# One stream of strips for the end of a four-layer image model on Trainium2

## The chip, the cores and the metric

The kernel runs on one core of a Trainium2 chip. A core has a matrix engine (TensorE, PE in the profile), a vector engine (VectorE, DVE), an activation engine (ScalarE, ACT), a general one (GpSimd, POOL) and a sync engine (SyncE, SP) that here only issues transfers. Each works through its own queue in order; waits between them go through semaphores. TensorE writes its results to PSUM, here in banks of 512 fp32 columns; all else lies in SBUF, and large tensors in DRAM. The metric is device microseconds of one execution. Before the change the median of three runs is 26510.6 us (26507.2 to 26526.69).

## The reference

The input x has 8 images of 64 x 64 positions and 192 channels. Four layers run one after the other, each with a residual. The last two and the end of the second are what matters:

```python
def _gn(v, G=32, eps=1e-5):
    ...
    m = jnp.mean(g, axis=(1, 2, 4), keepdims=True)
    s = jnp.var(g, axis=(1, 2, 4), keepdims=True)
    return ((g - m) / jnp.sqrt(s + eps)).reshape(v.shape)

def _ss2d(...):                       # layer 1
    ...
    y = out_y[:, 0] + inv_y[:, 0] + wh_y + invwh_y
    ...
    y = (y - mu) * jax.lax.rsqrt(var + 1e-05) * out_norm_w + out_norm_b
    y = y * jax.nn.silu(z)
    return jnp.einsum('bhwd,cd->bhwc', y, out_proj_w)

x = x + _L1_conv_ref(_gn(x), ...)
x = x + _L2_conv_ref(_gn(x), L2_conv_w, L2_conv_b)
x = x + _L3_conv_ref(_gn(x), L3_conv_w, L3_conv_b)
```

Layers 2 and 3 are depthwise 3 x 3 convolutions (each channel has nine taps of its own), of the input normalised over an image and a group of six channels. All is fp32.

## The kernel before

Channels lie on partitions: 192 are two tiles (ct) of 96, the 384 inner channels of layer 1 three tiles (o) of 128. An image has 4096 positions, worked in strips of 512, that is eight image rows (NCH = 8 strips per image, 64 in all). layer0 is layer 0; layer1 calls layer1_in (projection, convolution), layer1_scan (the selective scan in four directions, whose results y go to DRAM) and layer1_out; layers23 is layers 2 and 3. layer0, layer1_in and layer1_scan have a written order: inside every_engine the instructions of the four engines stand as the code emits them, and together runs Python generators in turns, each to its next yield. layer1_out and layers23 are not under it; a scheduler orders them. SP's order is a scheduler's everywhere.

layer1_out takes a strip at a time. It loads four y (L1140), adds them (L1142 and L1144 on VectorE, L1143 on POOL), normalises each row (norm_rows, from L116: bn_stats, Sqrt, subtract and multiply, transposes L137, scale and bias L138), projects the normalised input again for the gate (L1152, Silu L1159), multiplies (L1160), projects out (L1164), adds the residual (L1167) and takes the statistics for layer 2 (L1168). The result x2 goes to DRAM from POOL's queue (L1169). The tables of Sqrt and Silu are in different sets, so ScalarE loads tables twice per strip.

layers23 takes an image at a time. Per layer: group_norm_affine (two tiny matmuls, Sqrt), a normalised copy of the whole image (L1207), then conv3x3 per channel tile. In conv3x3 the three taps with dx = 0 are matmuls with diagonal matrices (L52, L57), the residual a matmul with the identity (L54); ScalarE evicts each strip with the bias (L64), and then VectorE adds the six other taps, each over the whole image (L71). For layer 3, bn_stats run over the finished layer 2 (L1202). At the end the image is turned back by transposes (L1220), copied (L1222, L1224) and stored (L1225).

Of the kernel before, what the change touches and what calls it, by code (L numbers as in the profile page):

```python
# [10 lines left out]
AF = mybir.ActivationFunctionType  # L11
ALU = mybir.AluOpType
PSUM = bass.MemoryType.PSUM
# [3 lines left out]
L = H * W  # L17
CP, CT = 96, 2
DIN = 384
# [19 lines left out]
def img(t, ct):  # L39
    return t[:, ct, :].rearrange("p (h w) -> p h w", w=W)  # L40


def conv3x3(nc, psum, src, dst, w, bias, diag, nct, ident, resid=None):


    rows = NJ // W
    P = src.shape[0]
    for ct in range(nct):
        for r in range(H // rows):
            h0 = r * rows  # L50
            ps = mk(psum, [128, NJ], "mm")[:P]
            nc.tensor.matmul(ps, diag[:, ct, 1, :], src[:, ct, h0 * W : h0 * W + NJ], start=True, stop=False)  # L52
            if resid is not None:
                nc.tensor.matmul(ps, ident[:P, :P], resid[:, ct, h0 * W : h0 * W + NJ], start=False, stop=False)  # L54
            for dy in (-1, 1):
                lo, hi = max(h0, -dy), min(h0 + rows, H - dy)
                nc.tensor.matmul(  # L57
                    ps[:, (lo - h0) * W : (hi - h0) * W],
                    diag[:, ct, 1 + dy, :],
                    src[:, ct, (lo + dy) * W : (hi + dy) * W],  # L60
                    start=False,
                    stop=dy == 1,
                )
            nc.scalar.activation(dst[:, ct, h0 * W : h0 * W + NJ], ps, AF.Identity, bias=bias[:, ct : ct + 1])  # L64
        s, d = img(src, ct), img(dst, ct)
        for dy in (-1, 0, 1):
            for dx in (-1, 1):
                h0, h1 = max(0, -dy), H - max(0, dy)
                w0, w1 = max(0, -dx), W - max(0, dx)
                tap = 3 * (dy + 1) + dx + 1  # L70
                nc.vector.scalar_tensor_tensor(  # L71
                    d[:, h0:h1, w0:w1],
                    s[:, h0 + dy : h1 + dy, w0 + dx : w1 + dx],
                    w[:, ct, tap : tap + 1],
                    d[:, h0:h1, w0:w1],
                    ALU.mult,
                    ALU.add,
                )


# [33 lines left out]


def norm_rows(nc, pool, psum, xt, ident, out, lw, lb):  # L116

    P, nct = out.shape[0], out.shape[1]
    nt = xt.shape[1]
    st = mk(pool, [128, nt, 6], "ln_st")  # L120
    mv = mk(pool, [128, nt, 2], "ln_mv")
    rs = mk(pool, [128, nt], "ln_rs")
    for i in range(nt):
        nc.vector.bn_stats(st[:, i, :], xt[:, i, :])
        nc.vector.bn_aggr(mv[:, i, :], st[:, i, :])
    nc.vector.tensor_scalar(rs, mv[:, :, 1], EPS, None, ALU.add)
    nc.scalar.activation(rs, rs, AF.Sqrt)
    nc.vector.reciprocal(rs, rs)
    for i in range(nt):
        nc.vector.tensor_scalar(  # L130
            xt[:, i, :], xt[:, i, :], mv[:, i, 0:1], rs[:, i : i + 1], ALU.subtract, ALU.mult
        )
    for g in range(nt // 4):
        for ct in range(nct):
            ps = mk(psum, [128, NJ], "tp")[:P]
            for j in range(4):
                nc.tensor.transpose(ps[:, j * 128 : (j + 1) * 128], xt[:, 4 * g + j, ct * P : (ct + 1) * P], ident)  # L137
            nc.scalar.activation(  # L138
                out[:, ct, g * NJ : (g + 1) * NJ],
                ps,  # L140
                AF.Identity,
                bias=lb[:, ct : ct + 1],
                scale=lw[:, ct : ct + 1],
            )
# [571 lines left out]
def layer1(ctx: ExitStack, tc, a, dr, x1, mv1, x2, mv2, cst):  # L716
# [34 lines left out]
    layer1_out(tc, load, w_in, normed, yk, x2, mv2, cst)  # L751
# [372 lines left out]
@with_exitstack  # L1124
def layer1_out(ctx: ExitStack, tc, load, w_in, normed, yk, x2, mv2, cst):

    nc = tc.nc
    ident = cst[0]
    onw, onb = load("onw", [DP, DT]), load("onb", [DP, DT])
    w_out = load("w_out1", [DP, DT, C])  # L1130
    po = ctx.enter_context(tc.tile_pool(name="o1", bufs=2))
    pt = ctx.enter_context(tc.tile_pool(name="t1", bufs=4, space=PSUM))
    for b in range(B):
        stt = mk(po, [CP, CT, NCH, 6], "stt")
        for ch in range(NCH):
            t0 = ch * NJ
            yin = []
            for k in range(K1):
                v = mk(po, [128, NJ // 128, DIN], "yin", bufs=8)
                nc.sync.dma_start(v, yk[b][k][t0 : t0 + NJ, :].rearrange("(t q) d -> q t d", q=128))  # L1140
                yin.append(v)
            nc.vector.tensor_tensor(yin[0], yin[0], yin[1], ALU.add)  # L1142
            nc.gpsimd.tensor_tensor(yin[2], yin[2], yin[3], ALU.add)  # L1143
            nc.vector.tensor_tensor(yin[0], yin[0], yin[2], ALU.add)  # L1144
            yn = mk(po, [DP, DT, NJ], "yn")
            norm_rows(nc, po, pt, yin[0], ident, yn, onw, onb)
            xt, gx = normed(po, b, ch)
            zs = mk(po, [DP, DT, NJ], "zs")
            for o in range(DT):
                ps = mk(pt, [128, NJ], "tp")  # L1150
                for ct in range(CT):
                    nc.tensor.matmul(  # L1152
                        ps,
                        w_in[:, ct, DIN + o * 128 : DIN + (o + 1) * 128],
                        gx[:, ct, :],
                        start=ct == 0,
                        stop=ct == CT - 1,
                    )
                nc.scalar.activation(zs[:, o, :], ps, AF.Silu)  # L1159
            nc.vector.tensor_tensor(zs, zs, yn, ALU.mult)  # L1160
            for ct in range(CT):
                ps = mk(pt, [128, NJ], "tp")[:CP]
                for o in range(DT):
                    nc.tensor.matmul(  # L1164
                        ps, w_out[:, o, ct * CP : (ct + 1) * CP], zs[:, o, :], start=o == 0, stop=o == DT - 1
                    )
                nc.vector.tensor_tensor(xt[:, ct, :], xt[:, ct, :], ps, ALU.add)  # L1167
                nc.vector.bn_stats(stt[:, ct, ch, :], xt[:, ct, :])  # L1168
            nc.gpsimd.dma_start(x2[b][:, :, ch * NJ : (ch + 1) * NJ], xt)  # L1169
        for ct in range(CT):  # L1170
            nc.vector.bn_aggr(mv2[:, b, ct, :], stt[:, ct, :, :])


@with_exitstack
def layers23(ctx: ExitStack, tc, a, x2, mv2, out, cst):
    nc = tc.nc
    ident, _, _, _, grp = cst
    wp = ctx.enter_context(tc.tile_pool(name="w2", bufs=1))
    ws, bs, dgs = [], [], []
    for i in (2, 3):  # L1180
        w = mk(wp, [CP, CT, 9], f"w{i}")
        nc.sync.dma_start(w, a[f"L{i}_w"])
        bt = mk(wp, [CP, CT], f"b{i}")
        nc.sync.dma_start(bt, a[f"L{i}_b"])
        ws.append(w)
        bs.append(bt)
        dgs.append(make_diag(nc, wp, w, CT, ident, f"dg{i}"))
    big = ctx.enter_context(tc.tile_pool(name="big2", bufs=5))
    small = ctx.enter_context(tc.tile_pool(name="small2", bufs=2))
    psum = ctx.enter_context(tc.tile_pool(name="ps2", bufs=4, space=PSUM))  # L1190
    for b in range(B):
        xc = mk(big, [CP, CT, L], "x")
        for ct in range(CT):
            nc.sync.dma_start(xc[:, ct, :], x2[b][:, ct, :])
        mv = mv2[:, b, :, :]
        for i in range(2):
            if i:
                st = mk(small, [CP, CT, NCH, 6], "st")
                mv = mk(small, [CP, CT, 2], "mv")
                for ct in range(CT):  # L1200
                    for ch in range(NCH):
                        nc.vector.bn_stats(st[:, ct, ch, :], xc[:, ct, ch * NJ : (ch + 1) * NJ])  # L1202
                    nc.vector.bn_aggr(mv[:, ct, :], st[:, ct, :, :])
            sc, nb = group_norm_affine(nc, small, psum, mv, grp)
            xn = mk(big, [CP, CT, L], "x")
            for ct in range(CT):
                nc.scalar.activation(  # L1207
                    xn[:, ct, :], xc[:, ct, :], AF.Identity, bias=nb[:, ct : ct + 1], scale=sc[:, ct : ct + 1]
                )
            xo = mk(big, [CP, CT, L], "x")  # L1210
            conv3x3(nc, psum, xn, xo, ws[i], bs[i], dgs[i], CT, ident, resid=xc)
            xc = xo
# [99 lines left out]
```

## Time and profile before

| | |
|---|---|
| median of three runs | 26510.6 us |
| the profiled execution | 26508.04 us |
| its span, first to last instruction | 26506.2 us |
| mean granted TensorE clock over it | 0.942 |
| busy: PE, DVE, ACT, POOL | 90%, 84%, 76%, 66% |
| last operation of the scan on VectorE | about 23664 us |
| last strip of layer1_out done | about 24959 us |

The profile is of one execution. In a line of groups stand the source line, engine and operation, the tiles written and read, the shapes and the number of instructions, then busy time, mean ns of one, and the idle time of the engine just before them with what ended it. A line of waits has who waited, for whom, the total in us, how often, and the longest. A line of the timeline has the start and the length in us and how many instructions were merged; the bracket is the idle time before it. An fp32 matmul of 512 columns shows as two records. PEclk is the clock that TensorE was granted, as a share of full speed; DMA is the mean busy share of the 16 DMA engines.

### The profile page before, as it was taken

The numbers are of one execution on the slowest core, as the hardware profiler recorded it, in microseconds if no ns is written. First come the engines' busy times: TensorE is split into PE (matmuls) and PEld (weight loads), VectorE is DVE, ScalarE is ACT, GpSimd is POOL, SyncE is SP. The second block draws the span as 40 slices with busy tenths as digits, with TensorE's granted clock in tenths as the row PEclk, the third lists the DMA queues.
The fourth block names the chain that finished last, engine by engine and source line by source line (L and its number), as shares of the span: only waits on it lengthen the run. The fifth ranks groups of instructions, "written<-read, shape, count | busy, mean of one in ns | idle before, by whom it ended". The sixth has DMA issues, their size and how long they took to land.

```text
span 26506.2 us, 442347 instructions
## 1 busy us (share of the span) xinstructions
PE 23817.3 (90%) x156160; PEld 18514.6 (70%) x156160; DVE 22196.4 (84%) x25001; ACT 20110.0 (76%) x40019; POOL 17618.6 (66%) x18396
## 2 busy tenths in 40 slices
PE   7888888887799999999999999999999999987766
PEld 4444444444478888888888888888888888863322
DVE  6777777655589999999999999999999999986566
ACT  4555555433379999999999999999999999984322
POOL 2222222210079999999999999999999999972100
PEclk8888888888899999999999999999999999998878
DMA  1111111112233333333333333333333333346411
GB/s 55 42 43 43 42 43 42 34 44 89 90 103 97 94 102 96 95 101 96 96 100 98 94 101 97 96 99 98 95 99 99 95 98 97 96 137 198 126 34 29
DMA packets 1461962, 2275.55 MB, mean 86 GB/s; under 512 B 247181, under 2 KB 773133, under 8 KB 1458202
## 3 DMA queue, kind: packets, MB, share of 16 engines
q1 hardware_dynamic: 1445402, 2196.90, 28.2%
q0 software_dynamic: 14336, 50.34, 0.5%
q8 instruction: 1232, 20.19, 0.3%
q14 instruction: 992, 8.13, 0.1%
HBM read 1811.37 MB, written 435.42 MB: 85 GB/s over the span
## 4 chain that ended last, share of the span: by engine, by line
PE 36%; ACT 29%; DVE 13%; POOL 13%; issue 6%; DMA 2%; POOLq 0%; SPq 0%; DVEq 0%; ACTq 0%
ACT dA L1039 12%; POOL hc L1089 10%; PE pd L1045 6%; ACT sb L1023 6%; PE yt L978 5%; DVE h L1080 5%; ACT bd L1023 4%; PE y L643 3%; PE fc L677 3%; DVE x L71 2%; DVE u L823 2%; PE mm L793 2%; DMA yin<-y 2%; PE pd L1047 2%; PE mm L399 2%
## 5 line engine op out<-in xcount | busy, mean ns | idle before, releaser
L1089 POOL TENSOR_TENSOR hc<-h,bc 128x512 f32<-128x512 f32 x12288 | 15425.9, 1289 | 488.7 <-DVE h L1080 342.0
L1080 DVE TENSOR_TENSOR_SCAN h<-dA,st,pd 128x512 f32<-128x512 f32 x10752 | 12949.9, 1263 | 530.9 <-PE pd L1045 369.4
L1039 ACT ACTIVATE dA<-dl,A_logs 128x512 f32<-128x512 f32 x12288 | 8787.0, 715 | 46.9 <-DVE h L1080 39.6
L978 PE MATMUL yt<-sq,hc 128*128 128x128 f32 x49152 | 7488.5, 275 | 198.8 <-POOL hc L1089 97.3
L1045 PE MATMUL pd<-bd,dut 128*128 128x128 f32 x49152 | 6582.1, 277 | 254.4 <-DVE h L1080 232.1
L1045 PEld LDWEIGHTS pd<-bd,dut 128*128 128x128 f32 x49152 | 5969.2, 192 | 610.3 <-PE yt L978 343.0
L978 PEld LDWEIGHTS yt<-sq,hc 128*128 128x128 f32 x49152 | 5668.1, 141 | 642.1 <-POOL hc L1089 623.3
L1023 ACT ACTIVATE sb<-dut,xt 128x384 f32<-128x384 f32 x8192 | 4763.5, 606 | 1.1 <-DVE dut L964 1.0
L1047 PE MATMUL pd<-sq,sb 128*128 128x128 f32 x24576 | 3739.5, 275 | 9.1 <-DVE h L1080 0.2
L1047 PEld LDWEIGHTS pd<-sq,sb 128*128 128x128 f32 x24576 | 2820.9, 141 | 480.6 <-DVE dl L951 380.8
L1023 ACT ACTIVATE bd<-sq,xt 128x128 f32<-128x128 f32 x8192 | 3011.1, 393 | 0.0
L1080 DVE TENSOR_TENSOR_SCAN h<-dA,pd 128x512 f32<-128x512 f32 x1536 | 1772.6, 1204 | 114.8 <-PE pd L1045 75.6
L71 DVE SCALAR_TENSOR_TENSOR x<-x,w,x 96x3969 f32<-96x3969 f32 (+1 forms) x192 | 838.3, 4366 | 488.6 <-ACT x L64 485.6
L538 POOL TENSOR_TENSOR xdt<-xb,dtv 128x384 f32<-128x384 f32 x256 | 220.7, 862 | 1365.5 <-ACT xb L532 1365.5
L800 POOL COPY xa<-xa 128x192 f32<-128x192 f32 x56 | 19.9, 356 | 1387.9 <-ACT xa L797 1387.9
L413 POOL COPY halo<-raw 128x12 f32<-128x12 f32 x64 | 12.8, 201 | 1380.8 <-ACT raw L403 1380.8
L304 DVE SCALAR_TENSOR_TENSOR x<-xs,cpe_w,x 96x504 f32<-96x504 f32 (+1 forms) x1024 | 899.4, 878 | 30.2 <-ACT x L292 20.4
L823 DVE SCALAR_TENSOR_TENSOR u<-xa,conv_w,u 128x504 f32<-128x504 f32 x1152 | 850.1, 743 | 63.5 <-ACT u L817 25.1
L937 PE MATMUL mm<-xs,w_dt 13*128 13x512 f32 x1536 | 863.0, 641 | 1.8 <-DVE dl L951 1.0
L677 PE MATMUL fc<-ff,fc_w 128*96 128x512 f32 x1536 | 858.9, 676 | 2.7 <-DVE xo L680 2.7
L1091 POOL COPY st<-h 128x3 f32<-128x3 f32 x4096 | 821.8, 201 | 0.0
L793 PE MATMUL mm<-g,w_in 96*128 96x512 f32 x768 | 487.5, 769 | 333.4 <-ACT g L739 332.9
(234 smaller groups left out, 26955.9 us busy)
## 6 DMA issues: line engine op xcount, KB each, us to landing
bc<-bcd SPq DMA_DIRECT2D x4096, 256.0 KB
yin<-y SPq DMA_DIRECT2D x256, 768.0 KB
csb<-csd SPq DMA_DIRECT2D x256, 384.0 KB
dut<-ut SPq DMA_DIRECT2D x128, 768.0 KB
y<-ys SPq DMA_DIRECT2D x128, 768.0 KB
dut<-ut SPq DMA_DIRECT2D x256, 384.0 KB
y<-ys SPq DMA_DIRECT2D x256, 384.0 KB
xt<-x1d SPq DMA_DIRECT2D x128, 384.0 KB
```

The costliest lines, as they stand in the source:

```text
L71: nc.vector.scalar_tensor_tensor(d[:, h0:h1, w0:w1], s[:, h0 + dy : h1 + dy, w0 + dx : w1 + dx], w[:, ct, tap : tap + 1], d[:, h0:h1, w0:w ...
L304: nc.vector.scalar_tensor_tensor(d[:, :, w0:w1], s[:, dy : dy + R, w0 + dx : w1 + dx], w[:, ct, tap : tap + 1], d[:, :, w0:w1], ALU.mult, ...
L677: nc.tensor.matmul(ps, f2w[:, o, ct * CP : (ct + 1) * CP], ff[:, o, :], start=o == 0, stop=o == 5)
L793: nc.tensor.matmul(ps, w_in[:, ct, o * 128 : (o + 1) * 128], g[:, ct, :], start=ct == 0, stop=ct == CT - 1)
L823: nc.vector.scalar_tensor_tensor(uv[:, o, :, w0:w1], tv[:, o, dy : dy + R, w0 + dx : w1 + dx], cw[:, o, tap : tap + 1], uv[:, o, :, w0:w1] ...
L978: nc.tensor.matmul(yt[:, t * 128 : (t + 1) * 128], src[:, t * 128 : (t + 1) * 128], mat, is_transpose=mat is ident, start=first and t == 0 ...
L1023: nc.scalar.activation(v, src, AF.Copy, scale=m["xt"][:, t, 1 + R1 + n : 2 + R1 + n])
L1039: nc.scalar.activation(dA, ready[s]["dl"][:, o, :], AF.Exp, scale=aneg[:, k, o, n : n + 1])
L1045: nc.tensor.matmul(dst, ready[s]["dut"][:, t, cols], brows[g, t], start=True, stop=True)
L1047: nc.tensor.transpose(dst, brows[g, t][:, cols], ident)
L1080: nc.vector.tensor_tensor_scan(h[:, o, rev], decay.pop(j)[:, rev], turned.pop(j)[:, rev], 0.0 if first else st[:, o, n : n + 1], ALU.mult, ...
L1089: nc.gpsimd.tensor_tensor(hc, h[:, o, :], held[g], ALU.mult)
```

## The change

layer1_out and layers23 become one function, tail, in the written order. It runs 64 + 20 steps. In step s four generators (five where an image begins) take turns: project(s - 1) is the second half of layer1_out for a strip, sums(s) the first half of the next, convolve(2, s - 10) and convolve(3, s - 20) are layers 2 and 3 of earlier strips. Every transfer is issued by SP.

sums normalises the rows on ScalarE, with 1/sqrt from Ln and Exp and one correction on VectorE (rsqrt) in place of Sqrt and a reciprocal.

Layers 2 and 3 work on a strip with one row above and one below (load_rows). No normalised copy is made. affine runs once per image and layer: it multiplies the taps by the scale, adds one to the middle tap (the residual), and puts what the mean contributes into the bias; rows outside the image are filled with the mean, and the first and last column get a correction on VectorE. Four taps are matmuls, the three with dx = 0 and (0, +1); the five others stay on VectorE, per strip. The statistics for layer 3 are taken per strip, and x3, the result of layer 2, goes to DRAM and comes back.

```diff
-def conv3x3(nc, psum, src, dst, w, bias, diag, nct, ident, resid=None):
...
-def norm_rows(nc, pool, psum, xt, ident, out, lw, lb):
...
-    layer1_out(tc, load, w_in, normed, yk, x2, mv2, cst)
+    x2 = [mk(dr, [CP, CT, L], f"x2d{b}") for b in range(B)]
+    x3 = [mk(dr, [CP, CT, L], f"x3d{b}") for b in range(B)]
+    tail(tc, a, load, w_in, normed, yk, x2, x3, out, cst)
...
+def tail(ctx: ExitStack, tc, a, load, w_in, normed, yk, x2, x3, out, cst):
...
+    def bank(tag):
+        return mk(psum, [128, NJ], tag, bufs={"tp": 2, "mm": 3, "cv": 3}[tag])
...
+    TAPS = (1, 4, 7, 5)
...
+    def sums(s):
...
+        y = yin.pop(s)
+        nc.vector.tensor_tensor(y[0], y[0], y[1], ALU.add)
+        nc.gpsimd.tensor_tensor(y[2], y[2], y[3], ALU.add)
+        for _ in range(4):
+            yield
+        nc.vector.tensor_tensor(y[0], y[0], y[2], ALU.add)
+        yield
...
+        for i in range(NB):
+            nc.vector.bn_stats(st[:, i, :], y[0][:, i, :])
+            nc.vector.bn_aggr(mv[:, i, :], st[:, i, :])
+            yield
+        nc.vector.tensor_scalar(ve, mv[:, :, 1], EPS, None, ALU.add)
+        yield
+        tc.keep_in_program_order(nc.scalar.preload_act_table_set("natural_log_exp_and_others"))
+        rsqrt(nc, pool, ve, rs, "rs")
+        nc.vector.scalar_tensor_tensor(nm, mv[:, :, 0], -1.0, rs, ALU.mult, ALU.mult)
+        yield
+        for i in range(NB):
+            nc.scalar.activation(
+                y[0][:, i, :], y[0][:, i, :], AF.Identity, bias=nm[:, i : i + 1], scale=rs[:, i : i + 1]
+            )
+        rows[s] = y[0]
+        yield
+
+    def project(s):
...
+        for o in range(DT):
+            pt = bank("tp")
+            for t in range(NB):
+                nc.tensor.transpose(pt[:, t * 128 : (t + 1) * 128], v[:, t, o * 128 : (o + 1) * 128], ident)
+            yield
+            nc.scalar.activation(yn[:, o, :], pt, AF.Identity, bias=onb[:, o : o + 1], scale=onw[:, o : o + 1])
+        for o in range(DT):
+            ps = bank("mm")
...
+            yield
+            nc.scalar.activation(zs[:, o, :], ps, AF.Silu)
+            yield
+            nc.vector.tensor_tensor(zs[:, o, :], zs[:, o, :], yn[:, o, :], ALU.mult)
...
+        for ct in range(CT):
+            ps = bank("mm")[:CP]
             for o in range(DT):
...
+                nc.tensor.matmul(ps, w_out[:, o, ct * CP : (ct + 1) * CP], zs[:, o, :], start=o == 0, stop=o == DT - 1)
+                yield
+            nc.vector.tensor_tensor(xt[:, ct, :], xt[:, ct, :], ps, ALU.add)
+            nc.vector.bn_stats(stats[2, b][:, ct, r, :], xt[:, ct, :])
+        nc.sync.dma_start(x2[b][:, :, r * NJ : (r + 1) * NJ], xt)
+        yield
...
+    def affine(i, b):
...
+        for ct in range(CT):
+            nc.scalar.activation(dgi[:, ct, :, :], dg[:, ct, :, :], AF.Copy, scale=sc[:, ct : ct + 1])
+            nc.vector.tensor_tensor(dgi[:, ct, 1, :], dgi[:, ct, 1, :], IDC, ALU.add)
+            nc.vector.tensor_scalar(wi[:, ct, :], w[:, ct, :], sc[:, ct : ct + 1], None, ALU.mult)
+            nc.vector.tensor_scalar(edge[:, ct, :], ws[:, ct, :], nb[:, ct : ct + 1], None, ALU.mult)
...
+    def convolve(i, s):
...
+        for ct in range(CT):
+            ps = bank("cv")[:CP]
...
+            for j, tap in enumerate(TAPS):
...
+                nc.tensor.matmul(
+                    pv[:, :, w0:w1],
+                    dgi[:, ct, j, :],
+                    sv[:, dy : dy + R, w0 + dx : w1 + dx],
+                    start=j == 0,
+                    stop=j == len(TAPS) - 1,
+                    skip_group_check=True,
+                )
+                if j % 2:
+                    yield
+            nc.scalar.activation(y[:, ct, :], ps, AF.Identity, bias=cb[:, ct : ct + 1])
+            yield
+            nc.vector.tensor_scalar(yv[:, :, 0:1], yv[:, :, 0:1], edge[:, ct, 0:1], None, ALU.add)
+            nc.vector.tensor_scalar(yv[:, :, W - 1 : W], yv[:, :, W - 1 : W], edge[:, ct, 2:3], None, ALU.add)
+            for tap in range(9):
+                if tap in TAPS:
+                    continue
...
+                nc.vector.scalar_tensor_tensor(
+                    yv[:, :, w0:w1],
+                    sv[:, dy : dy + R, w0 + dx : w1 + dx],
+                    wi[:, ct, tap : tap + 1],
+                    yv[:, :, w0:w1],
+                    ALU.mult,
+                    ALU.add,
+                )
+                yield
+            if i == 2:
+                nc.vector.bn_stats(stats[3, b][:, ct, r, :], y[:, ct, :])
+        if i == 2:
+            nc.sync.dma_start(x3[b][:, :, r * NJ : (r + 1) * NJ], y)
+            return
+        yield
+        ot = mk(pool, [128, NB, C], "ot")
+        for g in range(NB // 2):
+            ps = bank("tp")
+            for j in range(2):
...
+                    nc.tensor.transpose(ps[:, c0 : c0 + CP], y[:, ct, t : t + 128], IDC)
+            yield
+            nc.scalar.copy(ot[:, 2 * g : 2 * g + 2, :], ps[:, 0 : 2 * C].rearrange("p (j c) -> p j c", j=2))
+        nc.sync.dma_start(out[b].rearrange("(g j p) c -> g p j c", p=128, j=NB)[r], ot)
+        yield
+
+    LAG2, LAG3 = NCH + 2, 2 * NCH + 4
+    with every_engine(tc):
+        fetch(0)
+        for s in range(len(strips) + LAG3):
+            fetch(s + 1)
+            load_rows(2, s + 1 - LAG2)
+            load_rows(3, s + 1 - LAG3)
+            threads = [project(s - 1), sums(s), convolve(2, s - LAG2), convolve(3, s - LAG3)]
...
+            together(*threads)
```

## The prediction

> **What bounds it now.** I read the busy shares in 40 slices first: the 13th to the 35th, the selective scan, have all four engines at nine tenths, and the change does not touch them. Only the last four or five slices, from the end of the scan (about 23664 us) on, are at issue. The table of windows splits them:
>
> ```profile
> core 0: us, PE busy (x) PEld busy (x) DVE busy (x) ACT busy (x) POOL busy (x), PEclk, DMA share, GB/s
> 23664.00:24959.00 1295.00, 933.20 (x2322) 401.11 (x2322) 795.08 (x1360) 525.95 (x706) 272.76 (x133) 0.85 0.62 195
> 24959.00:26506.00 1547.00, 984.28 (x2622) 411.40 (x2622) 967.26 (x526) 326.61 (x368) 0.42 (x1) 0.80 0.12 33
> ```
>
> The rows are layer1_out (1295 us, 20 per strip of 512 tokens) and layers23 (1547 us, 193 per image), 2842 us together. No engine is above 74% in either. Whose wait it is, by the waits of the two stretches:
>
> ```profile
> POOL yin L1143 <- DMA yin<-y: 515.0, 57, 14.6
> DVE zs L1160 <- ACT zs L1159: 103.3, 48, 6.8
> ...
> DVE x L71 <- ACT x L64: 485.6, 17, 44.2
> PE mm L102 <- DVE mv L1203: 288.0, 8, 36.0
> ```
>
> In the first stretch transfers and a chain through all engines take turns. In the second the engines alternate: VectorE idles 485.6 us while TensorE and ScalarE fill half an image, TensorE idles 288 us while VectorE finishes it. Hence the granted clock of 0.80 to 0.85. The rows for the sum:
>
> ```profile
> L71 DVE SCALAR_TENSOR_TENSOR x<-x,w,x 96x3969 f32<-96x3969 f32 x128 | 556.1, 4344 | 487.4 <-ACT x L64 485.6
> L823 DVE SCALAR_TENSOR_TENSOR u<-xa,conv_w,u 128x504 f32<-128x504 f32 x990 | 730.5, 743 | 37.2 <-ACT u L817 4.1 <-DVE u L823 0.9
> L1167 DVE TENSOR_TENSOR xt<-xt,tp 96x512 f32<-96x512 f32 x116 | 77.8, 670 | 27.0 <-PE tp L1164 27.0
> L64 ACT ACTIVATE x<-mm,b 96x512 f32<-96x512 f32 x256 | 175.0, 683 | 672.7 <-PE mm L57 672.7
> ```
>
> and TensorE's own timeline, where one burst (12 records are six fp32 matmuls of 512 columns) shows both clocks:
>
> ```profile
> 24221.74 5.39 PE L1164 MATMUL tp<-zs,w_out 128*96 128x512 f32 x12 [2.48 <-DVE zs L1160]
> ...
> 24230.79 8.78 PE L1152 MATMUL tp<-g,w_in 96*128 96x512 f32 x12 [1.67 <-DVE ln_mv L125]
> ```
>
> A matmul is 0.86 us at full clock, 1.7 at half.
>
> **Part by part: work per strip.** Taken away: the normalised copy (L1207, 32 x 3.79 us ScalarE), the residual matmuls, the separate bn_stats pass of layer 3 (it moves to the strip), whole-image tiles. Added: one more tap on TensorE (four matmuls per 96 channels, as many as now with the residual), five taps instead of six on VectorE, edge corrections, folded weights once per image, and a round trip of x3 through DRAM.
>
> *Taps on VectorE.* Now 192 operations, 838 us. After: 64 strips x 2 layers x 2 x 5 = 1280. L823 has this shape (63 of 64 columns, 8 rows) at 743 ns, and twelve in a row take 9.18 us, so 0.77 each: 985 us. One sixth of the taps goes, but short operations cost 147 us more.
>
> *VectorE per strip*: sums 2 x 1.76 (L1142), 4 x 0.67 for bn_stats and bn_aggr, six small ones at 0.19: 7.3. Projection 3 x 0.69 (a third of L1160 plus its start), 2 x 0.74 (L1167 by start to start), 2 x 0.6: 4.8. Layer 2: 2 x (0.4 edges + 5 x 0.77 + 0.6 statistics) = 9.7; layer 3 8.5. Of the edge operations (96x8, strided) there is no row: between 0.16 (the 96x2 ones of the group norm) and 0.34 (L857, 176 columns), taken near the first at 0.2; the ends are -20 and +70 us over the tail. **30.2 us** against 27.5 now (1762/64).
>
> *TensorE per strip at full clock*: 12 matmuls of the projection 10.3, 16 of the taps 13.8, 12 plus 8 transposes 2.3: 26.4. ScalarE about 15, its two table loads per strip (62 + 62 of 1283 ns now) staying two. POOL 3.6. So VectorE is longest, and 64 x 30.2 = 1933 would be a gain of 900 us, if nothing made it wait.
>
> **What makes it wait: the written order.** The order in which the changed program's instructions stand on each engine shows a ring. TensorE's queue has a step's eight output transposes (they need the last tap of layer 3, nearly VectorE's last operation of the step) ahead of the next step's first taps; VectorE has add, then the edges of layer 2, which wait for those taps' eviction. Nothing on TensorE can pass. From VectorE's last tap at 0, for a full step:
>
> - TensorE has had nothing for 10 us and is at half clock: output transposes to 1.8 (eight take 1.49 at half clock), four transposes once the bank is copied out to 2.7, first two taps of layer 2 to 6.1, of layer 3 to 8.8, transposes 9.3, last two taps of layer 2 11.0. Eviction (L64) 11.9.
> - VectorE meanwhile does statistics and one add, 2.4 us, and idles 9.5.
> - Then it runs its other 27.8 us: first taps of both layers (0.6 waiting for layer 3), second add, nine pairs of taps with bn_stats and products between them, a wait of 0.6 for Ln and Exp, residual adds; the products zs are early enough for TensorE, which ends at 30. VectorE's last tap: 11.9 + 27.8 + 1.2 = **41 us**.
>
> [...] six bursts of the trace lost 1.7 to 3.4, mean 2.7. [...] I take the trace.
>
> **Steps.** 84 steps, as layer 2 follows the strips by 10 and layer 3 by 20:
> - 10 with sums and projection: VectorE 12, TensorE 11.6; the binding thing is 3.84 MB per strip at about 240 GB/s, between 195 (row above) and the 287 of its best slice: 16 (14 to 19.7). 160 us.
> - 10 with layer 2: no output transposes, no ring; VectorE 21.7 and 4.7 MB: 23.5. 235 us.
> - 44 full: 41. 1804 us. 5.6 MB per step are 137 GB/s: no bound.
> - 1 of 33, then 9 with both convolutions: ring to 10.3, VectorE 17.5, 0.6: 28.5. 290 us.
> - 10 with layer 3 alone: ring to 8.7, VectorE 8.5, hand-overs 0.6: 17.8. 178 us.
> - 16 foldings (bn_aggr to weights): on VectorE four small operations behind a TensorE matmul that stands behind layer 3's taps, a Ln and Exp behind a table load, thirteen small ones: 2 + 1.8 + 2.7, partly in the ring's wait: 6 each, from 3 if hidden to 9. 96 us. ScalarE's two extra loads per folding lie beside VectorE.
> - Start: 18 us until the first add as now, 5 for diagonals (L90 0.19 each); last output 5. 28 us.
>
> Sum 2791 against 2842: **51 us less**. 26506 - 51 = 26455 of span; the profiled execution took 26508, the median is 26511, so the same number serves.
>
> *Queues.* SP takes all transfers, also the x2 store that POOL issued (64 x 0.62 us). Per step: four y loads at 2.3 us issue, six others below 0.9, 14 of 41 us. The stores wait for VectorE's end of step; queued behind them are the halo loads of the step after next and y loads two steps ahead, so a full step covers them. If that cover went, a halo load (0.49 MB, an estimate of 2.5 us at 195 GB/s) would lie in the ring: up to 160 us, unlikely. DVE and POOL together: an add of 3.6 us per step, layer 0's taps under POOL run at 844 to 742: below 0.5 us, left out.
>
> **Rivals.**
> 1. *The clock holds* (out of 63 ring steps, TensorE at full rate): ring 8.2 instead of 11.9, 3.7 x 63 = 233: 26222. For: bursts after waits of 2.48 us ran full (5.39). Against: the pauses here are 10 us. Chance 0.18.
> 2. **Slower**: the half rate lasts twice as long, 10.8 us[...]. Place: the ring. Price: another 2.7 x 63 = 170: 26625. It decides from 0.8 us per step, where the gain is gone. For: 8.78 us bursts came after transposes and a pause of 1.67 only. Against: conv bursts after 36 us idle were full within 6.5. Chance 0.20.
> 3. *Transfers bind the first 20 steps* at 195 GB/s: 19.7 and 24: +42: 26497, no change. For: POOL's 515 us on yin now. Against: y loads are up to two strips ahead. Chance 0.15.
>
> That the order is not what the code says is out: it stands so on TensorE and VectorE.
>
> **Numbers.** Forecast 0.47, 26455, its own range 26390 to 26530. About 0.2% (53 us) is what this kernel's runs can tell from no change, and the forecast sits there. Faster: 0.30 of the forecast, 0.18, and 0.05 of rival 3: 0.53. Same: 0.15, 0.02, 0.09: 0.26. Slower: 0.02, 0.18, 0.01: 0.21. Range 26215 to 26640, from rival 1 to rival 2.
>
> **What would show it.** VectorE about 2010 us busy in the tail, the taps at 0.74 to 0.77; full steps of 41 us with one idle of 9 to 10 us on VectorE before the edge operation, released by ScalarE's eviction; TensorE idle 10 us before the output transposes; granted clock near 0.84 there. Steps of 37 mean rival 1, of 44 rival 2. It is wrong if VectorE's idle is elsewhere, say behind a y or halo load, or if taps cost clearly more than 0.77.

## The result and the profile after

The changed kernel takes 26403.1 us (median of 5, 26391.9 to 26406.8) against 26515.3 (median of 5, 26507.2 to 26526.7) for the kernel before on the same chip: a ratio of 0.9956, 95% interval 0.9941 to 0.997. It is 112 us faster where 51 were forecast. The kernel before was also timed beside the experiments below, at 26510 and 26513 us, so that their times can be set beside these. The profiled execution has a span of 26401.1 us. Line numbers below are those of the changed kernel: L1107, L1108 and L1111 are the three sums of the four directions (L1108 on POOL), L1259 the eviction of the taps from PSUM, L1261 and L1262 the edge corrections, L1268 VectorE's taps, L1290 the output transposes.

The scan ends about 9 us later than before (23673 instead of 23664); I have no cause for that and it is below what the runs can tell. The rest, 2842 us before, is 2728 now. This is the table of windows of the changed kernel, with the same columns as in the prediction; the rows are the steps with sums and projection, those with layer 2 as well, the full ones, those with both convolutions alone, and those with layer 3 alone:

```profile
23693.00:23886.00 193.00, 135.81 (x335) 58.91 (x336) 136.34 (x249) 108.95 (x162) 45.76 (x12) 0.81 0.72 230
23886.00:24145.00 259.00, 219.10 (x534) 89.07 (x533) 234.95 (x442) 132.80 (x200) 35.75 (x10) 0.89 0.62 187
24145.00:25949.00 1804.00, 1358.33 (x3371) 570.46 (x3369) 1353.24 (x2583) 684.25 (x1073) 152.65 (x42) 0.86 0.46 135
...
25990.00:26230.00 240.00, 155.28 (x364) 63.11 (x363) 150.18 (x318) 42.91 (x74) 0.00 (x0) 0.79 0.21 62
26230.00:26401.00 171.00, 105.54 (x238) 43.76 (x236) 84.13 (x165) 28.68 (x52) 0.00 (x0) 0.73 0.16 46
```

The full steps hold two thirds of the tail, and in them neither VectorE nor TensorE is busy for much more than 75% of the time. So they wait for each other, as forecast. Step by step, from one first sum to the next, beside the forecast (16 foldings of 6 us put where they fall):

| part | forecast | measured | |
|---|---|---|---|
| start to the first sum | 23 | 20 | -3 |
| 10 steps of sums and projection, 1 folding | 166 | 193 | +27 |
| 10 with layer 2, 2 foldings | 247 | 259 | +12 |
| 44 full steps, 10 foldings | 1864 | 1809.5 | -54 |
| the last projection | 33 | 34.6 | +2 |
| 9 with both convolutions, 2 foldings | 269 | 239 | -30 |
| 10 with layer 3, 1 folding; last output | 189 | 173 | -16 |
| sum | 2791 | 2728 | -63 |

The waits of the changed kernel in 1500 us of full steps (total, times, longest):

```profile
DVE y L1261 <- ACT y L1259: 234.4, 52, 10.4
PE tp L1290 <- DVE y L1268: 232.2, 36, 7.8
```

VectorE waits at the edge operation for the eviction and TensorE at the output transposes for the last tap, the two ends of one ring. One turn of it, from the timeline of the changed kernel (start, duration, engine, line, idle before and its releaser):

```profile
25210.04 1.38 DVE L1268 SCALAR_TENSOR_TENSOR y<-x,wi,y 96x504 f32<-96x504 f32 x2
25211.56 1.35 PE L1290 MATMUL tp<-sq,y 96*128 96x96 f32 x7 [6.14 <-DVE y L1268]
...
25213.75 5.79 PE L1249 MATMUL cv<-x,dgi 96*96 96x512 f32 x8
...
25219.82 3.57 PE L1249 MATMUL cv<-x,dgi 96*96 96x512 f32 x8
...
25221.72 0.68 ACT L1259 ACTIVATE y<-cv,acb 96x512 f32<-96x512 f32 x1 [0.93 <-PE cv L1249]
...
25222.44 0.23 DVE L1261 TENSOR_SCALAR y<-y,edge 96x8 f32<-96x8 f32 x1 [8.76 <-ACT y L1259]
```

The last tap ends at 25211.4, and the first edge operation starts 11.0 us later. In between stand the output transposes, two taps of each layer, the second pair and the eviction. The same eight records of L1249 take 5.79 us in the first burst and 3.57 in the second: the clock is at half for most of the first. The granted clock says the same, in the column behind the five engines (0.50, then 1.00):

```profile
25208.00:25218.00 10.00, 6.43 (x16) 3.42 (x17) 5.65 (x8) 3.04 (x5) 0.00 (x0) 0.50 0.69 204
25219.80:25223.30 3.50, 3.50 (x11) 1.37 (x10) 0.82 (x3) 1.46 (x2) 0.00 (x0) 1.00 0.89 256
```

This turn is one of the longer ones. Over the full steps the first burst takes from 3.6 to 6.1 us, 5.1 in the mean. In each of them the clock is at half when the transposes behind TensorE's pause start, and it is full again 3.5 to 8.5 us later.

Over the 32 full steps without a folding from the 22nd strip on, the way from last tap to edge operation is 10.7 us (forecast 11.9). VectorE waits 8.4 us at the edge operation (forecast 9.5) and idles 9.5 us per step in all (forecast 10.7, with its two waits of 0.6). TensorE's pause ahead of the output transposes is 6.3 us (forecast 10). A step is 40.0 us (forecast 41).

One thing in the timeline was not in the forecast. The same kernel, one stretch of a full step on VectorE and POOL:

```profile
25021.05 0.55 DVE L1116 BATCH_NORM_STATS2 st<-yin 128x6 f32<-128x384 f32 x1
25021.14 3.43 POOL L1108 TENSOR_TENSOR yin<-yin,yin 128x1536 f32<-128x1536 f32 x1 [37.78 <-DVE zs L1159]
25021.63 0.18 DVE L1117 BATCH_NORM_AGGREGATE mv<-st 128x2 f32<-128x6 f32 x1
25021.73 4.03 DVE L1268 SCALAR_TENSOR_TENSOR y<-x,wi,y 96x504 f32<-96x504 f32 x2
```

Two taps, elsewhere in the step 1.36 us, take 4.03 here: they end 1.2 us behind the end of POOL's add (25024.57), the first of them 0.5 us behind it, so the first stood still until POOL was all but done. Two statistics operations, one begun just before the add and one under it, took their usual time. The group of taps shows it over the whole run (busy total, mean ns; the median is 733, the longest 3974):

```profile
L1268 DVE SCALAR_TENSOR_TENSOR y<-x,wi,y 96x504 f32<-96x504 f32 x1280 | 1017.3, 831 | 12.6
```

### The profile page after: what moved, and what is told of

Its sections match the earlier page's. It is cut to its first block, busy times and chain, and to the rows that moved or that the text cites. A ratio compares the mean times of both kernels' runs of the same rounds, so it can differ in the third digit from the quotient of the medians.

```text
span 26401.1 us, 445286 instructions
## 1 busy us (share of the span) xinstructions
PE 23910.9 (91%) x156160; PEld 18544.3 (70%) x156160; DVE 22425.3 (85%) x26934; ACT 20270.1 (77%) x40529; POOL 17597.2 (67%) x18332
## 4 chain that ended last, share of the span: by engine, by line
PE 36%; ACT 29%; DVE 16%; POOL 12%; issue 6%; DMA 0%; SPq 0%; POOLq 0%; DVEq 0%; ACTq 0%
ACT dA L968 12%; POOL hc L1018 10%; ACT sb L952 6%; PE pd L974 6%; PE yt L907 5%; DVE h L1009 5%; ACT bd L952 4%; DVE y L1268 3%; PE y L570 3%; PE fc L604 3%; DVE u L752 2%; PE cv L1249 2%; PE mm L722 2%; PE pd L976 2%; PE mm L326 2%
## 5 line engine op out<-in xcount | busy, mean ns | idle before, releaser
L1108 POOL TENSOR_TENSOR yin<-yin,yin 128x1536 f32<-128x1536 f32 x64 | 234.2, 3659 | 1946.6 <-DMA yin<-y 1440.2
L1249 PE MATMUL cv<-x,dgi 96*96 96x512 f32 (+1 forms) x2048 | 1037.7, 656 | 7.5 <-ACT x L1238 7.5
L1268 DVE SCALAR_TENSOR_TENSOR y<-x,wi,y 96x504 f32<-96x504 f32 x1280 | 1017.3, 831 | 12.6
```

The source lines that it names most:

```text
L1249: nc.tensor.matmul(pv[:, :, w0:w1], dgi[:, ct, j, :], sv[:, dy : dy + R, w0 + dx : w1 + dx], start=j == 0, stop=j == len(TAPS) - 1, skip_g ...
L1268: nc.vector.scalar_tensor_tensor(yv[:, :, w0:w1], sv[:, dy : dy + R, w0 + dx : w1 + dx], wi[:, ct, tap : tap + 1], yv[:, :, w0:w1], ALU.mu ...
```

## The experiments

My theory after this reading had three parts: the ring sets the step (9 us of VectorE's time each), the half clock in it costs 2 to 3 us, and POOL's add takes 3.2 us from VectorE besides. The rivals were that transfers or the engines' own work set 40 us and the waits only show it, and that the long taps are an artefact of the records or lie in waits anyway.

**Break the ring.** The output transposes, copies and store of a strip move from the end of their step into the next one. (The expectation calls it the store of x3; it is the store of the finished output.)

```diff
+        done[s] = y
         yield
+    def give(s):
+        ...
+        y = done.pop(s)
+        for _ in range(5):
+            yield
         ot = mk(pool, [128, NB, C], "ot")
...
-            threads = [project(s - 1), sums(s), convolve(2, s - LAG2), convolve(3, s - LAG3)]
+            threads = [project(s - 1), sums(s), convolve(2, s - LAG2), convolve(3, s - LAG3), give(s - LAG3 - 1)]
```

> Computes the same. The output transposes of a strip, their copies and the store of x3 are written five places into the next step instead of at the end of their own, so that TensorE's queue has the first taps of the next strip ahead of them and VectorE's last tap of a step no longer releases its first edge operation of the next. THEORY (the ring TensorE - ScalarE - VectorE sets the step): VectorE's wait of about 10 us before the edge operation goes; a full step then is VectorE's own 30 us plus about 3 us in which it is held, 33 to 34 us instead of 40 (44 steps, -280); steps with both convolutions alone 18 to 19 instead of 26.5 (-70); steps with layer 3 alone about 10 instead of 17 (-70); in all about -420 against the changed kernel's 26403: 25980, and VectorE above 90% busy in the full steps. RIVAL (y loads, TensorE or ScalarE set the step of 40 us and VectorE's wait only shows it): the wait moves to another place, the full steps stay at 38 to 40 us, 26330 to 26420.

Measured: 25862.6 us, ratio 0.9754 (0.974 to 0.9769), 540 us below the changed kernel. The full steps are 31.0 us, the steps with both convolutions 15.9, those with layer 3 alone 9.3. From the timeline of this kernel, VectorE between two steps:

```profile
25022.28 0.68 DVE L1278 BATCH_NORM_STATS2 st<-y 96x6 f32<-96x512 f32 x1
25022.88 1.74 DVE L1107 TENSOR_TENSOR yin<-yin,yin 128x1536 f32<-128x1536 f32 x1
25024.99 0.23 DVE L1261 TENSOR_SCALAR y<-y,edge 96x8 f32<-96x8 f32 x1 [0.36 <-ACT y L1259]
```

The wait of 8.8 us in front of the edge operation is 0.4 here, and its full steps:

```profile
24145.00:25544.00 1399.00, 1246.05 (x3309) 514.34 (x3308) 1323.44 (x2528) 667.20 (x1056) 144.88 (x42) 0.93 0.58 171
```

VectorE is busy 95% of them, with the transfers at 171 GB/s where they had been at 135. So neither transfers nor TensorE had set the 40 us; the written order had. The rival falls. The gain is larger than I expected, because I took 33 to 34 us for a step from my own forecast of VectorE's work, which was too long (below).

**Keep the clock.** Matmuls whose result nobody reads fill TensorE's pause ahead of the output transposes.

```diff
+        spare = bank("mm")[:CP]
+        n = 9 if s + LAG3 <= len(strips) else 8 if s + LAG3 < len(strips) + LAG2 else 5
+        for _ in range(n):
+            nc.tensor.matmul(spare, dgi[:, 0, 1, :], x[:, 0, W : W + NJ], start=True, stop=True)
         ot = mk(pool, [128, NB, C], "ot")
```

> Adds 5 to 9 matmuls of 512 columns per step, whose result nobody reads, just ahead of the output transposes, where TensorE has nothing to do for 8 to 10 us; all else as in the changed kernel. THEORY (the half clock lengthens the ring): the transposes and first taps run at full clock, the ring is shorter by 2.3 to 3 us in each of 63 steps: -150 to -190, 26210 to 26255; VectorE's wait before the edge operation falls from 10.4 to about 7.7 us and the granted clock of the full steps rises from 0.86 to above 0.95. RIVAL 1 (something else than TensorE ends VectorE's wait last): clock up, time within 30 us of 26403. RIVAL 2 (the added matmuls are too long and hold the transposes back): 26450 or more.

Measured: 26288.1 us, ratio 0.9915 (0.99 to 0.9929): 115 us below the changed kernel, where 150 to 190 were expected. The timeline of this kernel around one turn of the ring:

```profile
24955.60 7.89 PE L1286 MATMUL mm<-x,dgi 96*96 96x512 f32 x18
...
24963.33 1.14 PE L1294 MATMUL tp<-sq,y 96*128 96x96 f32 x8
...
24965.20 3.60 PE L1249 MATMUL cv<-x,dgi 96*96 96x512 f32 x8
```

The first burst of taps now runs at full clock, 3.60 us instead of the 5.1 in the mean, and the granted clock in 1500 us of full steps is 0.97 instead of 0.85. Steps of 40.0 us become 37.6, those with both convolutions about 22.9 instead of 25 to 26, those with layer 3 alone 13.5 instead of 16.6. But of the eight steps of an image two gained nothing, the one between the two foldings and the one after them (the cause is open), so the mean over the full steps without a folding goes from 40.0 to 38.5 only. The half clock is real and worth 1.4 to 2.9 us per turn in the other six steps; its 115 us are about a fifth of what breaking the ring gave.

**POOL's add on VectorE.**

```diff
-        nc.gpsimd.tensor_tensor(y[2], y[2], y[3], ALU.add)
+        nc.vector.tensor_tensor(y[2], y[2], y[3], ALU.add)
```

> Computes the same. The second of the three adds that sum the four directions runs on VectorE, right behind the first, instead of on POOL; POOL has no arithmetic left in the tail. THEORY (while POOL's add of 3.6 us runs, one operation of VectorE stands still for about 3.2 us in each step): this goes; the added 1.75 us lies in VectorE's wait for the eviction, so full steps fall from 40 to about 37 us (-140), the steps before them gain 1 to 2 us each (-25): about 26240, and no tap lasts over 1 us. RIVAL (the long taps are an artefact of the records, or the held operation stood in VectorE's waits anyway): the step stays or grows by the 1.75 us: 26400 to 26520.

Measured: 26250.5 us, ratio 0.9901 (0.9886 to 0.9915), 153 us below the changed kernel, with 1.75 us more work per step on VectorE. The group of taps in the tail of this kernel:

```profile
L1268 DVE SCALAR_TENSOR_TENSOR y<-x,wi,y 96x504 f32<-96x504 f32 x1280 | 888.5, 730 | 12.7
```

129 us of the taps are gone and the mean is at the median. Full steps are 37.2 us, 2.85 shorter; the first twenty steps gain too, 16 us in the first ten and 18 in the second. The held time is shown, and it was real time.

**Both edits.** The first and the third kernel's edits together.

> Both edits of the first and the third of these kernels; computes the same. THEORY (ring and hold both cost, and with the ring broken VectorE is the bound): VectorE has no wait left to hide the added 1.75 us, so that the second edit is worth only 3.2 - 1.75 = 1.5 us per full step here, less than its 3.2 alone: full steps of 32 us, about -70 against the first of these kernels, 25910. If the two gains simply add up (-560), 25840; if the steps stop at 38 us with VectorE idle elsewhere, transfers or TensorE bind behind the ring: above 26300.

Measured: 25765.8 us, ratio 0.9718 (0.9702 to 0.9734), below both sums, because the ring alone had brought more than they took. Every full step without a folding is 29.5 us, 1.5 less than with the ring alone, as the first theory had it: with the ring broken the added 1.75 us has no wait to hide in. The steps without layer 3 gain as before, and so the second edit is worth 97 us here against 153 alone, where I had expected 70. The full steps of this kernel:

```profile
24145.00:25446.00 1301.00, 1174.70 (x3215) 492.64 (x3214) 1230.91 (x2514) 646.97 (x1030) 0.00 (x0) 0.95 0.61 181
```

VectorE and TensorE are busy 95% and 90%, and the granted clock is 0.95. This version is 745 us faster than the kernel before and 637 faster than the changed one.

**The stages apart.** What is the overlap of layer 1's end with layers 2 and 3 worth by itself?

```diff
-            stats[2, b] = mk(pool, [CP, CT, NCH, 6], "st2")
+            stats[2, b] = mk(pool, [CP, CT, NCH, 6], "st2", bufs=B)
...
-    LAG2, LAG3 = NCH + 2, 2 * NCH + 4
+    LAG2, LAG3 = len(strips) + 2, len(strips) + NCH + 4
```

> Computes the same. Layers 2 and 3 follow the strips of layer 1 by 66 and 76 steps instead of 10 and 20, so that layer 1's end runs alone, then layers 2 and 3; strips, taps and order within a step are those of the changed kernel, ring and POOL's add too. By the step lengths of the changed kernel: 64 steps of sums and projection at 16.5 (1056, 15 more to fill), 10 with layer 2 alone at 12 (120), 54 with both convolutions at 26 (1404), 10 with layer 3 at 17 (170), 16 foldings at 5 (80), 25 for start and end: 2870 against 2728 measured. THEORY (laying the stages over each other saves only 16.5 + 26 - 40 = 2.5 us per full step, because the ring keeps VectorE waiting in each): +140 us, 26545, no better than before the change. RIVAL 1 (the overlap brings the gain that the sum of the engines' work allows, 10 us and more per full step): above 26800. RIVAL 2 (overlap is worth nothing): 26380 to 26430.

Measured: 26601.1 us, ratio 1.0033 (1.002 to 1.0047): 198 us above the changed kernel, and 88 slower than the kernel before. The direction of the theory holds, though its sum was 56 us short. Steps of sums and projection take 17.7 us, 1.2 more than I had taken from the first ten of the changed kernel. So the overlap as written brings 198 us, more than the whole gain of the change. The trace also parts the rest: the last projection ends 1142 us after the first sum, against some 1277 before (1295 less the 18 until the first add); layers 2 and 3 alone, in strips, then take 1763 us against 1547 in half images. Taken by themselves, and with the ring in them, the strips of layers 2 and 3 made those layers slower.

**Apart, with the ring broken.**

> Computes the same. Layers 2 and 3 behind layer 1's end as in the kernel before this one, and the output transposes five places into the next step as in the first kernel. By measured steps: 64 at 16.5 and 15 to fill (1071), 10 at 12 (120), 54 with both convolutions at 15.9 as in the first kernel (859), 10 at 9.3 (93), foldings 80, 25: 2248, 480 less for breaking the ring than in the kernel before: 25920 to 25950. THEORY (the strips of layers 2 and 3 need the ring broken, overlap with layer 1 or not; the overlap itself is worth 60 to 80 us then): that. RIVAL (the ring matters only when sums and projection fill the step): 26400 or more.

Measured: 26021.1 us, ratio 0.9815 (0.98 to 0.983), 580 us below the kernel just before. Layers 2 and 3 alone now take 1185 us instead of 1763. From 25920 to 25950 was expected; the excess is again the sums and projection, 17.9 us per step. The ring costs as much with the stages apart (580 us) as with them overlapped (540), and the overlap is worth 198 us with the ring and 158 without. So one changes what the other is worth by 40 us only; the rival, that only full steps suffer, falls.

**Taps in alternation.** Starting from the kernel with both edits, the taps of a strip alternate between its two tiles.

```diff
-        for ct in range(CT):
...
-            for tap in range(9):
-                if tap in TAPS:
-                    continue
+        for tap in range(9):
+            if tap in TAPS:
+                continue
...
+            for ct in range(CT):
+                sv, yv = views[ct]
                 nc.vector.scalar_tensor_tensor(
```

> Computes the same. From the kernel with ring broken and POOL's add on VectorE (25766): the five taps of a strip alternate between its two tiles of 96 channels instead of finishing one tile first. THEORY (a tap that follows the one it adds to starts 0.77 us after it, one on another tile 0.65): ten taps of a strip of layer 3 alone stand in one chain of about 6.6 us instead of two of 3.84; 1 us in each of 10 last steps, nothing in the full steps, where two layers' taps alternate already: 25750 to 25765. RIVAL (the 0.77 is set by the shape or by layer 3 alone): chains at 0.77, no change or, since both tiles now wait for both evictions, slower by up to 20 us.

Measured: 25972.3 us, ratio 0.9797 (0.978 to 0.9813), 207 us slower than the kernel it starts from, and outside every expectation. In layer 3 alone, first the kernel with both edits, then this one:

```profile
25692.08 3.84 DVE L1268 SCALAR_TENSOR_TENSOR y<-x,wi,y 96x504 f32<-96x504 f32 x5
```

```profile
25900.79 6.62 DVE L1273 SCALAR_TENSOR_TENSOR y<-x,wi,y 96x504 f32<-96x504 f32 x10
```

The mechanism is as I had it: ten taps stand in 6.62 us (0.65 each), not in two chains of 3.84 (0.77). The loss comes from elsewhere. With the taps regrouped, the instructions of all threads fall differently into the queues, and the second group matmul of a folding comes to stand behind the full steps' taps on TensorE. From the timeline of this kernel:

```profile
24641.67 0.25 PE L1194 MATMUL tp<-aq,grp 96*96 96x2 f32 x2
...
24641.96 0.15 DVE L1196 TENSOR_SCALAR aq<-tp 96x2 f32<-96x2 f32 x1 [9.85 <-PE tp L1194]
```

VectorE waits 9.9 us for a matmul of 0.25. By the waits of the full steps (total, times, longest) it does so ten times; the list of the kernel with both edits has no such wait:

```profile
DVE aq L1196 <- PE tp L1194: 99.1, 10, 10.0
```

Steps with a folding take 46.8 us instead of 36.2, and ten of them are about 106 of the 207 us. The other full steps went from 29.5 to 31.0 in the mean (49 us); the cause of that stays open. Everything behind the last sum takes 49 us more. There VectorE waits 52 us for evictions instead of 18, and another 17 for the same group matmul.

## Why the prediction was right, and where its sum was off

The likeliest case is the one that happened: faster, by a ring at half clock, with transfers not binding in the full steps. Point by point:

- **The ring.** "VectorE's last tap: 11.9 + 27.8 + 1.2 = 41 us" was measured at 10.7 + 29.3 = 40.0, with a wait of 8.4 us (for 9.5) at the operation named, released by the engine named. Breaking it gave 540 us. The mechanism is shown; 11.9 was 1.2 us too long. TensorE's pause was 6.3 us and not 10, but the clock fell to half in it all the same.
- **The clock.** I took a loss of 2.7 us per turn from six bursts of the kernel before. The first burst takes 5.1 us in the mean and 3.60 with the pause filled, a loss of 1.5; the transposes ahead of it lose some 0.7 more (2.47 us in the turn shown, 1.80 with the pause filled). Together that is 2.2, half a microsecond below the forecast. Filling the pause gave 1.4 to 2.9 us in six full steps of eight and about 3 in a step with layer 3 alone. The clock was full again 3.5 to 8.5 us after the transposes began. The forecast's first burst was 6.1 us long, and this is most of the 1.2 us by which the ring was too long. TensorE's two rows in the prediction do not tie the half clock to the pause just before the burst: the one of 8.78 us stood behind an idle time of 1.67 us and the one of 5.39 behind a longer one, 2.48. Over layer1_out of the kernel before, the long pauses do: all 14 bursts of twelve records (L1152, L1164) behind an idle time of over 4 us took 6.9 to 8.4 us.
- **The taps.** "twelve in a row take 9.18 us, so 0.77 each: 985 us" is the term that was mis-sized. The row came from a chain in which each tap adds to the result of the last. In the full steps two layers' taps alternate, and there they stand at 0.65: six in 3.99 us. Twenty taps a step at 0.12 less are 2.4 us, over 100 us in the full steps alone. Where one layer runs alone, layer 2 in the second ten steps and layer 3 in the last, the 0.77 is back.
- **POOL's add.** "DVE and POOL together: ... below 0.5 us, left out" is the step that was wrong. It costs about 3 us of each full step: 2.85 in the third kernel, which pays no price for the moved add. I had looked at taps of layer 0 under POOL, 844 ns against 742, and taken their mean for the whole; the longest of those taps took 2.15 us. The kernel before had the sign in the very stage at issue. One of nine long operations there, of 1.76 us otherwise, with POOL's add beside it:

```profile
24855.27 3.42 POOL L1143 TENSOR_TENSOR yin<-yin,yin 128x1536 f32<-128x1536 f32 x1 [7.83 <-DMA yin<-y]
24855.42 4.88 DVE L1160 TENSOR_TENSOR zs<-zs,yn 128x1536 f32<-128x1536 f32 x1 [3.38 <-ACT zs L1159]
```

  There 50 of the 64 adds held no operation of VectorE, mostly because it waited anyway, which is why the group's median hid it; in the new order an add falls into VectorE's work in nearly every step. In the four rows of the changed kernel the first tap waits for the end of POOL's 3.43 us, as do all 42 taps of this trace that start under an add, while the two statistics operations pass (0.55 and 0.18 us), as do all 27 that start under one. Why some operations are held and others not, the runs don't show. The taps' gain of 2.4 us and this loss of about 3 nearly cancel, so "other 27.8 us" plus waits of 1.2 looked right at 29.3. Two errors of opposite sign made one good number. The same holds for VectorE's busy time in the tail: "about 2010 us" was measured at 1992, but some 180 of these are operations standing still for POOL. Both agreements are luck.
- **The first twenty steps** were 39 us longer than forecast, close to the 42 us of rival 3 (transfers), but not for its reason: 33 us went when POOL's add was moved, with the transfers left as they were. The first ten steps then still took 177 us for 166; their second step, where the pipeline fills, is 30.0 us long in the changed kernel and 28.8 in that one. (The 515 us that the rival leans on are of the stretch from 23700 to 24860 us; over all of layer1_out that wait is 539.8 us.)
- **The foldings** at 6 us: steps with one are 45.2 us against 40.0, so 5.2 in that step, and some of it in the step beside it.
- **The end**: steps with layer 3 alone at 16.6 instead of 17.8, with both convolutions at 25 to 26 instead of 28.5. Where both convolutions run, part of the excess is the taps' alternation. The rest I did not take apart.
- **The rivals.** Rival 1 (full clock) and rival 2 (half rate for 10.8 us) are both refused: in every full step the clock is at half when TensorE's pause ends, and it is full again 3.5 to 8.5 us later.

The larger thing that the prediction didn't ask was whether the ring had to be. By its own numbers VectorE's work of 30.2 us per strip would have meant a gain of 900 us, and of that it left 51. The ring was named as a cost and accepted as part of the change, though moving eight transposes past the next strip's taps lifts it and gives 540 us, more than the overlap of the stages brings (198 with the ring, 158 without).

## What to carry to other kernels

When engines work through queues in a written order, look for two waits that face each other across a step (here VectorE's edge operation for TensorE, TensorE's output transposes for VectorE): put the work that nobody needs soon, such as an output, behind the first work of the next step, and the ring opens. Before counting an add on POOL as free, look at the longest VectorE operation beside it, not at the mean or the median of a group. And take the pitch of a chain from a row with the same dependence, not only the same shape; then look again at all the queues, because regrouping one thread moves the others' instructions too.

## What the runs showed of the hardware

- VectorE's scalar_tensor_tensor of 96x504 fp32 starts 0.77 us after the one whose result it adds to, and 0.65 us after one on another tile (five in 3.84 us, ten in 6.62).
- While POOL adds two SBUF tiles (128x1536 fp32, mostly 3.4 to 3.8 us), a tap on VectorE stands still: all 42 that began under an add in the changed kernel ended 0.54 us behind it. bn_stats and bn_aggr pass: 27 began under an add and took their usual 0.2 to 0.7 us. With the add moved to VectorE the 1280 taps took 129 us less. Three tensor_scalar operations of the changed kernel (L96, L1119, L1205) that began under an add took 3.4 us instead of about 0.2.
- In pauses of 4.8 to 7.8 us on TensorE, in the full steps of the changed kernel, the granted clock fell to half (0.50), and it was full again 3.5 to 8.5 us after work resumed. The first burst behind the pause took 5.1 us in the mean; with the pause filled it took 3.60.
